# Batches 1 to 7 get their transposed tokens from VectorE blocks and SBUF transfers, and DRAM scratch is laid out in longer rows

## The chip, the cores and the metric

The kernel runs on one core of a Trainium2 chip. The engines named here are TensorE (PE; PEld is its weight load), VectorE (DVE), ScalarE (ACT), GpSimd (POOL) and SyncE (SP), which issues the DMAs of this kernel. The metric is the device time of one execution in microseconds (us), as a median over runs. Data is rearranged on the host before and after the launch, and this is not timed.

## What is computed

The input x has 8 batches of 2048 tokens with 512 features, in float32. The reference, cut to what matters:

```python
xn = _layernorm(x, axis=-1)
q = (xn @ Wq.T + bq).reshape(B, M, 8, 8)
k = (xn @ Wk.T + bk).reshape(B, M, 8, 8)
v = (xn @ Wv.T + bv).reshape(B, M, 8, 64)
scores = einsum('bmhd,bnhd->bhmn', q, k) / sqrt(8)
scores = where(scores >= 0, scores, 0.2 * scores)
out = einsum('bhmn,bnhd->bmhd', softmax(scores), v)
s = gamma * out + xn
base = xn @ W.T                      # feed-forward
ret = ...                            # top-1 of 4 gates per token, its softmax weight
res = sum over 4 experts of ret * (xn @ Wd_i.T) @ Wu_i.T
return x + s * silu(base + res)
```

## The kernel before

A batch's 2048 tokens are cut into 4 blocks of 512 (`BLK`). Two kinds of background work are done per block. `project_block` makes q, k and v from the normalized tokens and writes them to DRAM scratch (QS, KS, VS). `lift_block` makes the feed-forward part and writes it to GS. The main work is attention: for each batch, block of queries and pair of heads (a unit `s`, 128 of them) the inner loop takes 16 steps (`CH`), one per chunk of 128 keys. One step computes scores (`score`, L641), the leaky slope on ACT (`leaky`, L652), subtracts the row maximum with a matmul of two rows (`less_max`, L658), takes the exponential (`exp`, L670), finds maxima for the unit after next (`max_unit`, L586 on PE and L597 on DVE), and adds the exponentials up on POOL (`add_up`, L702). Weighing the values (`weigh`, L682) is put off in a list `last`.

The order of all engines' instructions is the order in which the Python program emits them. Background work consists of generators. Three queues hold them: the ending of a unit, the row shift, and `behind()`, which walks through the list of jobs (projections of batch b + 1 and lifts of batch b, interleaved). Each yield has a label. In each step `half_full()` chooses between weighing up to two chunks and moving a generator on: HOLD means that matmuls into a bank are being accumulated, and two of them fill a step; TINY work goes beside one weighing; WAIT is work that only follows up. A planner gives every job a cost (A1 for a projection, A2 for a lift, MM = 0.86 for one 512-column matmul) and due times (`due_at`), and `spend` counts what has been done; background work is held back once it is 6.0 ahead of the due time. In the last batch `half_light()` does the same in another rhythm.

The tokens' way before. `load_x` brings a block to SBUF (`xt`, two buffers). `norm(b, n)` is a generator that computes the statistics on DVE (L304, L305), the scale and shift on POOL, and issues the first of four normalizations on ACT (L319, into `xn`). It is started one job ahead and moved on only in those steps of `half_full` in which no background matmul is due. `project_block` then transposes the block on PE with 16 matmuls of 128x128 against an identity (L370) in four groups `tp`; each group is copied to `xnT` by DVE (L373) and followed by the next normalization. After the key projection, `split_keys` writes KS and QS (L338, L343), and the normalized tokens XN and the transposed ones XT are stored to DRAM (L389, L390), all on SP. `lift_block` reads XT back (`fetch`, L328). `load_stacks(s + 2)` reads keys and queries in the first steps of a unit (L542, L548), and `max_unit` uses them from step 5 on, since it runs 16 + 11 chunks ahead (`LEAD`). `read_for_ending` reads GS, x and XN for one pair of heads (L713, L715, L716), and `ending` writes the result (L763).

Of the kernel before, what the change touches and what calls it, by code (L numbers as in the profile page):

```python
# [32 lines left out]
def fused_layer_kernel(  # L33
    ctx: ExitStack,
    tc: tile.TileContext,
    x: bass.AP,
    wqk: bass.AP,
# [34 lines left out]
    B, M, C = x.shape  # L72
    NC = C // 128
    NB = M // BLK
# [3 lines left out]
    xv = x.rearrange("b (n p t) c -> b n p t c", p=128, t=NT)  # L78
    ov = out.rearrange("b (n p t) c -> b n p t c", p=128, t=NT)
# [15 lines left out]
    KS = [tc.dram_tile([HEADS, 4, DQK, M], FP, name=f"KS{b}") for b in range(B)]  # L95
    VS = [tc.dram_tile([NPAIR, 128, CH, 128], FP, name=f"VS{b}") for b in range(B)]
    GS = [tc.dram_tile([NB, 128, NT, C], FP, name=f"GS{b}") for b in range(B)]
    XN = [tc.dram_tile([NB, 128, NT, C], FP, name=f"XN{b}") for b in range(B)]
# [6 lines left out]
    def load_x(b, n):  # L105
        xt = two.tile([128, NT, C], FP, name="xt")
        if (b, n) == (0, 0):
            for t in range(NT):
                nc.sync.dma_start(out=xt[:, t, :], in_=xv[b, n][:, t, :])
        else:  # L110
            nc.sync.dma_start(out=xt, in_=xv[b, n])
        xtiles[b, n] = xt
# [146 lines left out]

    def project(ps, wt, xnT):  # L260
        for c in range(NC):
            for part in pieces():
                if c or part.start:
                    yield HOLD
                nc.tensor.matmul(  # L265
                    ps[:, part],
                    lhsT=wt[:, c, :],
                    rhs=xnT[c][:, part],
                    start=(c == 0 and part.start == 0),
                    stop=(c == NC - 1 and part.stop == BLK),  # L270
                )
                spend(MM / len(pieces()))

    def token_major(ps, wt, xnT, t, more=False):
        for c in range(NC):
            for part in pieces():
                if c or part.start:
                    yield HOLD
                nc.tensor.matmul(  # L279
                    ps[:, part],  # L280
                    lhsT=xnT[c][:, t * 128 : (t + 1) * 128],
                    rhs=wt[:, c, part],
                    start=(c == 0 and part.start == 0),
                    stop=(c == NC - 1 and part.stop == BLK and not more),
                )
                spend(MM / len(pieces()))

    def columns(*tiles):
        return [a[:, c, :] for a in tiles for c in range(a.shape[1])]
# [8 lines left out]
    def norm(b, n):  # L298
# [17 lines left out]
        xn = two.tile([128, NT, C], FP, name="xn")  # L316

        def normalize(t):
            nc.scalar.activation(  # L319
                xn[:, t, :], xt[:, t, :], AF.Identity, bias=nmr[:, t : t + 1], scale=rstd[:, t : t + 1]  # L320
            )

        normalize(0)
        normed[b, n] = xn, normalize
# [6 lines left out]
    def split_keys(b, n, ps, hi, lo):  # L331
        nc.vector.tensor_tensor(
            hi.bitcast(I32), ps.bitcast(I32), hi_bits.to_broadcast([128, BLK]), ALU.bitwise_and
        )
        nc.vector.tensor_tensor(lo, ps, hi, ALU.subtract)
        tok = slice(n * BLK, (n + 1) * BLK)
        for j in range(4):
            nc.sync.dma_start(  # L338
                out=KS[b][:, j, :, tok],
                in_=(hi, lo)[j // 2][64:128, :],  # L340
            )
        for j in range(4):
            nc.sync.dma_start(  # L343
                out=QS[b][:, j, :, tok],
                in_=(hi, lo)[j % 2][0:64, :],
            )
# [14 lines left out]
    def project_block(b, n, prefetch):  # L361
# [3 lines left out]
        xn, normalize = normed.pop((b, n))  # L365
        xnT = two.tile([128, NC, BLK], FP, name="xnT")
        for t in range(NT):
            tp = bank([128, NC, 128], "tp")
            for c in range(NC):
                nc.tensor.transpose(tp[:, c, :], xn[:, t, c * 128 : (c + 1) * 128], ident)  # L370
            if t + 1 < NT:
                normalize(t + 1)
            nc.vector.tensor_copy(xnT[:, :, t * 128 : (t + 1) * 128], tp)  # L373
            spend(0.5)
            yield TINY if t + 1 < NT else FREE
        if prefetch:
            fetch(*prefetch)
        nxt = b * NB + n + 2
        if nxt < B * NB:
            load_x(nxt // NB, nxt % NB)  # L380

        ps = bank([128, BLK], "qkps")
        yield from project(ps, wqk_sb, columns(xnT))
# [5 lines left out]
        nc.sync.dma_start(out=XN[b][n], in_=xn)  # L389
        nc.sync.dma_start(out=XT[b][n], in_=xnT)  # L390
# [5 lines left out]
        for t in range(NT):  # L396
            ps = bank([128, C], "vps")
            yield from token_major(ps, wv_sb, columns(xnT), t)
            add_bias(vb, t, ps)
            yield FREE if prefetch or t + 1 < NT else TINY  # L400
# [4 lines left out]
    def lift_block(b, n, prefetch, cols=None):  # L405
# [3 lines left out]
        if not early:  # L409
            if (b, n) not in fetched:  # L410
                fetch(b, n)
            cols = columns(fetched.pop((b, n)))
# [70 lines left out]
        if early:  # L483
            yield EARLY
            fetch(b, n)
            cols = columns(fetched.pop((b, n)))
            if prefetch:
                fetch(*prefetch)
# [20 lines left out]
        g = one.tile([128, NT, C], FP, name="g")  # L509
        for t in range(NT):  # L510
# [7 lines left out]
            nc.vector.scalar_tensor_tensor(g[:, t, :], th, 1.0, ps, ALU.add, ALU.mult)  # L518
            yield SLOW if prefetch or t + 1 < NT else TINY
        nc.sync.dma_start(out=GS[b][n], in_=g)  # L520
# [11 lines left out]
    def load_stacks(s):  # L532
# [7 lines left out]
        for r in range(2):  # L540
            half = slice(2 * STK * r, 2 * STK * (r + 1))
            nc.sync.dma_start(  # L542
                out=kst[s % 3][half, :].bitcast(FP).rearrange("r (c p) -> r c p", p=128),
                in_=KS[b][2 * p : 2 * p + 2].rearrange("e j d (c r p) -> r (e j d) c p", r=2, p=128)[r],
            )
# [160 lines left out]
    def read_for_ending(s):  # L706
# [4 lines left out]
        cols = slice(p * 128, (p + 1) * 128)  # L711
        gs = two.tile([128, NT, 128], FP, name="gs")
        nc.sync.dma_start(out=gs, in_=GS[b][n][:, :, cols])  # L713
        xs = two.tile([128, 2, NT, 128], FP, name="xs")
        nc.sync.dma_start(out=xs[:, 0], in_=xv[b, n][:, :, cols])  # L715
        nc.sync.dma_start(out=xs[:, 1], in_=XN[b][n][:, :, cols])  # L716
        reads[s] = gs, xs

    def ending(s):

        b, p, n = where(s)
        cols = slice(p * 128, (p + 1) * 128)
# [40 lines left out]
        nc.sync.dma_start(out=ov[b, n][:, :, cols], in_=gs)  # L763


    A1, A2, LIFTED, KEYED, VALUED = 20 * MM + 2.0, 24 * MM + 3.7, 1.3, 13.8, 15.0
# [29 lines left out]
    def behind():  # L796
        jobs = [t for t in tasks if t[0]]
        for k, (f, b, n, _, _) in enumerate(jobs):
            g, bb, nn = (jobs[k + 1] if k + 1 < len(jobs) else (None, 0, 0))[:3]
            if g is project_block:  # L800
                stats[bb, nn] = norm(bb, nn)
# [44 lines left out]

    def half_full():
# [8 lines left out]
        if go_on():  # L856
            values(run)
            return
# [3 lines left out]
        if j is not None and state[j] == TINY:  # L862
            values(min(run, 1))
            go(j)
            ended[0] = True
        elif j is None or len(last) > MUCH - (state[j] != HOLD) or (ended[0] and run > 1):
            ended[0] = False
            for g in stats.values():
                next(g, None)
# [32 lines left out]
    with tc.manual_schedule():  # L902
# [5 lines left out]
        def normalize_all(own, n):  # L908
# [5 lines left out]
            nc.sync.dma_start(out=XN[0][n], in_=xn)  # L914

        def turn(n, own, between):

            xn, _ = normed.pop((0, n))
            if n < 2:
                full = two.tile([128, NC, BLK], FP, name="xnT")  # L920
                halves = [full[:, 0:2, :], full[:, 2:4, :]]
# [32 lines left out]
        def value(n, t):  # L954
            if t == 0:
                if n % 2:
                    spare = one.tile([128, NT, C], FP, name="g")
                    vbs[n] = spare.rearrange("p a (b d) -> p a b d", b=NT)
# [40 lines left out]
        for n in range(NB):  # L999
# [123 lines left out]
```

## Time and profile before

| what | us |
|---|---|
| median of three runs | 5593.18 |
| lowest and highest run | 5574.32, 5600.27 |
| span of the profiled execution | 5580.8 |
| TensorE busy in the span | 5338.6 |
| GpSimd busy | 4778.5 |
| ScalarE busy | 4448.0 |
| VectorE busy | 3672.4 |

The profiled execution has its span, from its first instruction to its last, as its own time; no other is given for it. It lies between the lowest and the highest run. The DMA engines are busy 35% of the span, and 615 MB move. In the profile a group of instructions has its line, engine, operation, output and inputs, shapes, count, busy time and the mean time of one in nanoseconds, and then the idle time of the engine before them with what ended it. A list of waits has the waiting engine and line, what released it, and the total us, the number of times and the longest.

### The profile page before, as it was taken

The page shows a single profiled execution, that of the slowest core. Times are in us where ns is not written, and L with a number is a line of the kernel's source. Part 1 is how long each engine was busy: PE and PEld are TensorE (multiplying, and loading weights), DVE is VectorE, ACT ScalarE, POOL GpSimd, SP SyncE. Part 2 cuts the span into 40 slices and gives each one's busy share as a digit, 9 for nine tenths or more (in the row PEclk, how much of TensorE's full clock was granted, in tenths as well). Part 3 has the DMA queues.
Part 4 walks back from the last instruction along what each step waited for, and adds up shares of the span by engine and source line. Part 5 has one row for each costly group of instructions (what it writes and reads, how often), then busy time and mean ns, then how long its engine had stood idle before and what let it go on. Part 6 is the DMA issues. An engine that isn't in the chain of part 4 may idle for free.

```text
span 5580.8 us, 78283 instructions
## 1 busy us (share of the span) xinstructions
PE 5338.6 (96%) x26258; PEld 1975.0 (35%) x26258; DVE 3672.4 (66%) x4990; ACT 4448.0 (80%) x8627; POOL 4778.5 (86%) x2906
## 2 busy tenths in 40 slices
PE   7999999999999999999999999999999999999998
PEld 3333333333333333333333333333333333333332
DVE  5665766667666666667667666676666667666663
ACT  1787888788887788878888788887788878888887
POOL 1887898889897889988899888898889988899898
PEclk9998999999998999999999999999999999999998
DMA  5333343334423343333432334323343242432221
GB/s 191 113 111 114 109 133 97 101 116 120 125 94 95 124 127 111 98 101 124 136 108 88 108 116 152 101 80 117 111 146 95 83 144 88 142 96 84 72 78 61
DMA packets 528265, 615.39 MB, mean 110 GB/s; under 512 B 44092, under 2 KB 438332, under 8 KB 491768
## 3 DMA queue, kind: packets, MB, share of 16 engines
q1 hardware_dynamic: 527864, 610.39, 35.1%
q8 instruction: 209, 3.42, 0.3%
q14 instruction: 192, 1.57, 0.1%
HBM read 407.88 MB, written 202.38 MB: 109 GB/s over the span
## 4 chain that ended last, share of the span: by engine, by line
PE 84%; ACT 8%; DMA 3%; DVE 2%; issue 1%; SPq 1%; POOL 0%; ACTq 0%; POOLq 0%; DVEq 0%
PE av L682 30%; PE sc L658 17%; PE zps L279 9%; PE vps L279 8%; PE mx L586 8%; ACT ex L670 5%; ACT sc L652 3%; DMA q_sb<-QS 2%; PE qkps L265 2%; PE pps L265 2%; PE dps L265 2%; PE atp L754 1%; PE dps L737 1%; PE tp L370 1%; DVE mxr L597 1%
## 5 line engine op out<-in xcount | busy, mean ns | idle before, releaser
L702 POOL TENSOR_TENSOR acc<-acc,ex 128x1024 f32<-128x1024 f32 x1792 | 4231.4, 2361 | 255.3 <-ACT ex L670 138.4
L597 DVE TENSOR_REDUCE mxr<-mx 128x2 f32<-128x1024 f32 x2030 | 2480.0, 1222 | 1209.7 <-PE sc L658 942.8
L670 ACT ACTIVATE ex<-sc 128x512 f32<-128x512 f32 x4096 | 2228.5, 596 | 951.8 <-PE sc L658 831.3
L652 ACT ACTIVATE sc<-sc 128x512 f32<-128x512 f32 x4096 | 2234.4, 591 | 17.9 <-PE sc L641 17.9
L682 PE MATMUL av<-ex,v_sb 128*64 128x512 f32 x8192 | 2140.3, 627 | 4.5 <-DVE avs L724 3.1
L658 PE MATMUL sc<-shift,ones_r 2*128 2x512 f32 x4096 | 1654.7, 462 | 77.7 <-ACT sc L652 65.8
L586 PE MATMUL mx<-k,q_sb 32*128 32x512 f32 x4096 | 1463.2, 453 | 66.3 <-DMA q_sb<-QS 62.4
L658 PEld LDWEIGHTS sc<-shift,ones_r 2*128 2x128 f32 x4096 | 694.8, 187 | 1542.3 <-ACT sc L652 1453.1
L641 PE MATMUL sc<-q_sb,k 32*128 32x512 f32 x4096 | 1036.4, 502 | 0.0
L682 PEld LDWEIGHTS av<-ex,v_sb 128*64 128x64 f32 x8192 | 468.6, 138 | 843.1 <-issue 819.5
L586 PEld LDWEIGHTS mx<-k,q_sb 32*128 32x128 f32 x4096 | 572.6, 187 | 90.5 <-issue 69.8
L279 PE MATMUL zps<-w_sb,xnT 128*128 128x512 f32 (+1 forms) x1120 | 529.0, 589 | 7.5 <-DMA xnT<-XT 7.5
L279 PE MATMUL vps<-wv_sb,xnT 128*128 128x512 f32 x960 | 477.1, 621 | 0.2
L702 POOL TENSOR_TENSOR acc<-ex 128x1024 f32<-128x1024 f32 x128 | 301.8, 2357 | 169.0 <-ACT ex L670 168.7
L641 PEld LDWEIGHTS sc<-q_sb,k 32*128 32x128 f32 x4096 | 385.4, 185 | 0.8 <-issue 0.8
L279 PEld LDWEIGHTS zps<-w_sb,xnT 128*128 128x128 f32 x1120 | 187.0, 190 | 234.9 <-issue 229.7
L279 PEld LDWEIGHTS vps<-wv_sb,xnT 128*128 128x128 f32 x960 | 164.5, 190 | 200.1 <-issue 198.7
L518 DVE SCALAR_TENSOR_TENSOR g<-th,zps 128x512 f32<-128x512 f32 x128 | 88.0, 688 | 185.0 <-ACT th L517 185.0
L611 POOL TENSOR_TENSOR ml<-m,big 128x8 f32<-128x8 f32 x128 | 26.2, 205 | 202.5 <-DVE m L610 196.3
L349 DVE TENSOR_TENSOR vb<-vps,bv_sb 128x512 f32<-128x512 f32 x120 | 82.9, 691 | 93.4 <-PE vps L279 93.2
L373 DVE COPY xnT<-tp 128x512 f32<-128x512 f32 x112 | 77.3, 690 | 97.5 <-PE tp L370 97.5
L265 PE MATMUL dps<-xnT,wd_sb 128*128 128x512 f32 (+1 forms) x280 | 134.4, 592 | 0.0
(124 smaller groups left out, 2717.7 us busy)
## 6 DMA issues: line engine op xcount, KB each, us to landing
v_sb<-VS SPq DMA_DIRECT2D x127, 1024.0 KB
k<-KS SPq DMA_DIRECT2D x256, 256.0 KB
XN<-xn SPq DMA_DIRECT2D x32, 1024.0 KB
q_sb<-QS SPq DMA_DIRECT2D x256, 128.0 KB
xnT<-XT SPq DMA_DIRECT2D x32, 1024.0 KB
GS<-g SPq DMA_DIRECT2D x32, 1024.0 KB
gs<-GS SPq DMA_DIRECT2D x128, 256.0 KB
xs<-in_x_dram SPq DMA_DIRECT2D x128, 256.0 KB
```

The lines of the kernel that those rows point to most:

```text
L265: nc.tensor.matmul(ps[:, part], lhsT=wt[:, c, :], rhs=xnT[c][:, part], start=(c == 0 and part.start == 0), stop=(c == NC - 1 and part.stop ...
L279: nc.tensor.matmul(ps[:, part], lhsT=xnT[c][:, t * 128 : (t + 1) * 128], rhs=wt[:, c, part], start=(c == 0 and part.start == 0), stop=(c = ...
L349: nc.vector.tensor_tensor(vb[:, :, t, :], ps.rearrange("p (h d) -> p h d", h=NPAIR), bv_sb.rearrange("p (h d) -> p h d", h=NPAIR), ALU.add,)
L518: nc.vector.scalar_tensor_tensor(g[:, t, :], th, 1.0, ps, ALU.add, ALU.mult)
L586: nc.tensor.matmul(parts[e], lhsT=q_sb[r, t * 128 : (t + 1) * 128], rhs=k_sb[r, kb // 2 * BLK : (kb // 2 + 1) * BLK], start=True, stop=True,)
L597: nc.vector.reduce_max(mxr[s][:, :, t, kb : kb + 1], mx, axis=AX.X)
L641: nc.tensor.matmul(sc[e], lhsT=k_sb[r, i // 2 * 128 : (i // 2 + 1) * 128], rhs=q_sb[r, :], start=True, stop=True,)
L652: nc.scalar.activation(sc[e], sc[e], AF.Prelu, alpha=SLOPE)
L658: nc.tensor.matmul(sc[e], lhsT=ones_r[r, :], rhs=shifts[s][r, :], start=False, stop=True, skip_group_check=True,)
L670: nc.scalar.activation(ex[:, e, :], sc[e], AF.Exp, scale=qscale)
L682: nc.tensor.matmul(avt[s][64 * e : 64 * e + DV, :], lhsT=v_sb[:, i, 64 * e : 64 * e + DV], rhs=ex[:, e, :], start=(i == 0), stop=(i == CH ...
L702: nc.gpsimd.tensor_tensor(acc[s], old, ex, ALU.add)
```

## The change

For batches 1 to 7 the tokens are no longer transposed on PE. `norm` normalizes in place (`xt`, now with three buffers). DVE transposes each group of 512 features in 32x32 blocks into a tile `xb`, which leaves each block in the wrong group of partitions. Sixteen DMAs from SBUF to SBUF, each from 32 partitions to 32, put the blocks in their place in `xnT`. The host lays out x so that the order of the tokens comes out right. `norm` is started two jobs ahead, and a new function `prepare` moves it on in more kinds of steps. The transfers wait until the job before the projection has begun. XN is then stored with four DMAs, and the next block is loaded at the end of `norm`. `project_block` finds its tokens ready and stores XT only after the third group of values.

In DRAM, KS keeps a row of 1024 keys together, GS and the output are split by pairs of heads, and x comes a second time (`xp`) in that order. XN is in token order. Key stores become eight DMAs in place of four, key loads four in place of two. The first batch still uses PE; its first two blocks stay in SBUF for the first two lifts, so that four half-block XT stores and two reads less are made. The planner's A1 falls by 2.0.

The diff, cut to its core:

```diff
-    KS = [tc.dram_tile([HEADS, 4, DQK, M], FP, name=f"KS{b}") for b in range(B)]
+    KS = [tc.dram_tile([4, HEADS * DQK, 2, M // 2], FP, name=f"KS{b}") for b in range(B)]
-    GS = [tc.dram_tile([NB, 128, NT, C], FP, name=f"GS{b}") for b in range(B)]
-    XN = [tc.dram_tile([NB, 128, NT, C], FP, name=f"XN{b}") for b in range(B)]
+    GS = [tc.dram_tile([NB, NPAIR, 128, NT, 128], FP, name=f"GS{b}") for b in range(B)]
+    XN = [tc.dram_tile([NB, BLK, C], FP, name=f"XN{b}") for b in range(B)]
...
+    def turned_columns(xnT):
+        by_c = xnT.rearrange("p a (c m) -> p c a m", c=NC)
+        return [by_c[:, c] for c in range(NC)]
...
-    def norm(b, n):
+    turn_at = [0]
+    def norm(b, n, job=0):
...
         normalize(0)
-        normed[b, n] = xn, normalize
+        if b == 0:
+            normed[b, n] = xt, normalize
+            return
+        xb = one.tile([128, 4, NC, NT, 32], FP, name="xb")
+        for t in range(NT):
+            yield
+            nc.vector.transpose(
+                xb[:, :, :, t, :].rearrange("p f c i -> p c f i"),
+                xt[:, t, :].rearrange("p (c f j) -> p c f j", c=NC, f=4),
+            )
+            if t + 1 < NT:
+                normalize(t + 1)
+        while turn_at[0] < job - 1:
+            yield
+        xnT = two.tile([128, NC, BLK], FP, name="xnT")
+        for a in range(4):
+            for f in range(4):
+                nc.sync.dma_start(
+                    out=xnT[32 * f : 32 * f + 32, a, :],
+                    in_=xb[32 * a : 32 * a + 32, f].rearrange("j c t i -> j (c t i)"),
+                )
+        fetched[b, n] = xnT
+        yield
+        for t in range(NT):
+            nc.sync.dma_start(
+                out=XN[b][n].rearrange("(a t i) c -> t a i c", a=4, t=NT)[t], in_=xt[:, t, :]
+            )
+        yield
+        nxt = b * NB + n + 2
+        if nxt < B * NB:
+            load_x(nxt // NB, nxt % NB)
...
     def split_keys(b, n, ps, hi, lo):
         for j in range(4):
-            nc.sync.dma_start(
-                out=KS[b][:, j, :, tok],
-                in_=(hi, lo)[j // 2][64:128, :],
-            )
+            keys = (hi, lo)[j // 2][64:128, :].rearrange("k (c r p) -> r k c p", r=2, p=128)
+            for r in range(2):
+                nc.sync.dma_start(
+                    out=KS[b][j, :, r, n * BLK // 2 : (n + 1) * BLK // 2].rearrange("k (c p) -> k c p", p=128),
+                    in_=keys[r],
+                )
...
     def project_block(b, n, prefetch):
         for _ in stats.pop((b, n)):
             pass
-        xn, normalize = normed.pop((b, n))
-        xnT = two.tile([128, NC, BLK], FP, name="xnT")
-        for t in range(NT):
-            tp = bank([128, NC, 128], "tp")
-            for c in range(NC):
-                nc.tensor.transpose(tp[:, c, :], xn[:, t, c * 128 : (c + 1) * 128], ident)
-            if t + 1 < NT:
-                normalize(t + 1)
-            nc.vector.tensor_copy(xnT[:, :, t * 128 : (t + 1) * 128], tp)
-            spend(0.5)
-            yield TINY if t + 1 < NT else FREE
+        xnT = fetched.pop((b, n))
+        cols = turned_columns(xnT)
         if prefetch:
             fetch(*prefetch)
-        nxt = b * NB + n + 2
-        if nxt < B * NB:
-            load_x(nxt // NB, nxt % NB)
...
-        nc.sync.dma_start(out=XN[b][n], in_=xn)
-        nc.sync.dma_start(out=XT[b][n], in_=xnT)
...
+            if t == 2:
+                nc.sync.dma_start(out=XT[b][n], in_=xnT)
...
     def lift_block(b, n, prefetch, cols=None):
         if early:
             yield EARLY
-            fetch(b, n)
-            cols = columns(fetched.pop((b, n)))
-            if prefetch:
-                fetch(*prefetch)
...
-        nc.sync.dma_start(out=GS[b][n], in_=g)
+        nc.sync.dma_start(out=GS[b][n].rearrange("h p t d -> p h t d"), in_=g)
...
     def load_stacks(s):
         for r in range(2):
-            half = slice(2 * STK * r, 2 * STK * (r + 1))
-            nc.sync.dma_start(
-                out=kst[s % 3][half, :].bitcast(FP).rearrange("r (c p) -> r c p", p=128),
-                in_=KS[b][2 * p : 2 * p + 2].rearrange("e j d (c r p) -> r (e j d) c p", r=2, p=128)[r],
-            )
+            for e in range(2):
+                h = 2 * p + e
+                nc.sync.dma_start(
+                    out=kst[s % 3][rows(r, e), :].bitcast(FP),
+                    in_=KS[b][:, h * DQK : (h + 1) * DQK, r, :],
+                )
...
-    A1, A2, LIFTED, KEYED, VALUED = 20 * MM + 2.0, 24 * MM + 3.7, 1.3, 13.8, 15.0
+    A1, A2, LIFTED, KEYED, VALUED = 20 * MM, 24 * MM + 3.7, 1.3, 13.8, 15.0
...
     def behind():
+        begun = set()
         for k, (f, b, n, _, _) in enumerate(jobs):
-            if g is project_block:
-                stats[bb, nn] = norm(bb, nn)
+            turn_at[0] = k
+            for m in (k + 1, k + 2):
+                if m < len(jobs) and jobs[m][0] is project_block and jobs[m][1:3] not in begun:
+                    begun.add(jobs[m][1:3])
+                    stats[jobs[m][1:3]] = norm(*jobs[m][1:3], m)
...
+    def prepare():
+        for g in stats.values():
+            if next(g, g) is not g:
+                break
     def half_full():
         if go_on():
             values(run)
+            prepare()
             return
...
         if j is not None and state[j] == TINY:
             values(min(run, 1))
             go(j)
+            prepare()
             ended[0] = True
         elif j is None or len(last) > MUCH - (state[j] != HOLD) or (ended[0] and run > 1):
             ended[0] = False
-            for g in stats.values():
-                next(g, None)
+            prepare()
             values(run)
```

## The prediction

> **What bounds the kernel now.** I read the page's busy shares first, then its list of line groups, then the waits of TensorE (PE), and last the busy time of single steps of the inner loop, because shares are averages over unlike steps.
>
> ```profile
> span 5580.8 us, 78283 instructions
> PE 5338.6 (96%) x26258; PEld 1975.0 (35%) x26258; DVE 3672.4 (66%) x4990; ACT 4448.0 (80%) x8627; POOL 4778.5 (86%) x2906
> ...
> L702 POOL TENSOR_TENSOR acc<-acc,ex 128x1024 f32<-128x1024 f32 x1792 | 4231.4, 2361 | 255.3 <-ACT ex L670 138.4
> ...
> L373 DVE COPY xnT<-tp 128x512 f32<-128x512 f32 x112 | 77.3, 690 | 97.5 <-PE tp L370 97.5
> ```
>
> PE is the fullest engine. GpSimd (POOL) is next: 2048 steps at 2.36 us are 4833 us, so no saving on PE goes much below some 4900. In the waits of PE only two entries are large and touched by the change, and one single wait:
>
> ```profile
> PE mx L586 <- DMA q_sb<-QS: 62.4, 18, 7.3
> PE tp L370 <- ACT xn L319: 47.0, 28, 1.7
> PE zps L279 <- DMA xnT<-XT: 7.5, 1, 7.5
> ```
>
> (Columns: total us, times, longest.) A step is one pass of the loop over key chunks; on PE it runs from one pair of score matmuls (L641) to the next. The first starts at 132.2 us, so the 2048 steps hold 5448.6 us. Busy time of six stretches (columns: length, then busy PE, PEld, DVE, ACT, POOL, clock, DMA share, GB/s):
>
> ```profile
> 574.00:576.54 2.54, 2.54 (x17) 0.88 (x17) 2.48 (x4) 2.11 (x5) 2.46 (x2) 1.00 0.03 3
> 1857.96:1860.18 2.22, 1.74 (x14) 0.56 (x12) 2.19 (x4) 1.75 (x5) 2.14 (x2) 1.00 0.04 4
> 366.59:370.84 4.25, 2.57 (x14) 1.10 (x15) 2.01 (x3) 4.25 (x8) 4.15 (x2) 1.00 0.46 177
> 382.13:384.39 2.26, 2.26 (x17) 0.92 (x16) 1.40 (x3) 1.73 (x5) 2.26 (x1) 1.00 0.38 112
> 384.39:387.01 2.62, 2.53 (x15) 1.09 (x14) 1.95 (x3) 2.62 (x6) 2.46 (x3) 1.00 0.07 13
> 412.84:420.40 7.56, 1.43 (x10) 0.68 (x6) 1.15 (x4) 0.99 (x2) 1.92 (x1) 0.71 0.99 255
> ```
>
> In order: a step with two chunks weighed (2.54 us); one with a single chunk and no other work (2.22); a block's first four transposes with two normalizations on ScalarE (ACT), 4.25; four transposes and no normalization, 2.26; four with one, 2.62; and a step that waits for q_sb with the DMA engines full. The reader is to see that the transposes hardly lengthen a step (2.26 against 2.22). What lengthens it is the normalization of 0.82 us on ACT, which is full in the third and fifth row, and the wait for it.
>
> **The change, part by part.** The sum is made against the span of 5580.8 us; the three timed runs have the median 5593.2 (5574 to 5600), so the span lies 12 below it and I carry differences over to the median.
>
> Transposes out. Over all steps of the trace, the 112 with tp transposes last 347.0 us: 28 with two normalizations 116.0 (4.14 each), 56 with one 162.6 (2.90), 28 with none 68.4 (2.44). Each also weighs one chunk. The 199 steps with one weighing alone average 2.28. If the 112 become such steps: 347.0 - 112 x 2.28 = 91.6 us less. The planner's cost A1 falls by 2.0 of 19.2, which moves the due times but adds no instruction; priced at 0, its effect on phases is in the DMA term.
>
> Normalizations moved. All 112 stay (0.82 us each, in place now) and go, one per call of prepare, to steps with weighings. ACT spends 2.1 to 2.2 us of a step on scores and exponentials. Lower end 0: a tanh of 0.60 us in a two-chunk step costs nothing (77 steps with it and 485 without, both median 2.54). Upper end 0.82 each (92 us), ACT having no slack. In the transpose steps one normalization costs 2.90 - 2.44 = 0.46. About half the calls fall in two-chunk steps like the tanh's, half in one-chunk steps; I take 0.25: +28 us.
>
> VectorE (DVE). Out go 112 copies of 0.69 us, in come 112 block transposes of 128x512. The trace has only 128x32, 0.201 us; ends are 0.68 (other operations over 512 elements) and 16 x 0.201 = 3.2. A copy of 128x32 takes 0.180 (L479), so the price grows as for other operations and I take 0.7: 0, beside PE work on an engine 66% busy. If that cover went, a DVE burst longer than a step would hold up mx. The g write in another order is like the add of bias (0.691 against 0.688): 0. The transposes wait for ACT's normalization of the call before, a step earlier; queued behind them is the row maximum mxr, for which the next mx waits.
>
> Queues. SP issues in order. A block's key split (from 400.23 us in the first projection) issues 4 KS, 4 QS, XN and XT stores at 0.5 to 1.6 us each until 408.1; only then come the loads of k (2.75) and q (2.79), which land at 419.4, while mx needs them at 413.3. That is the 6.1 us wait, with XN and XT, 1 MB each, ahead of the loads on engines at a share of 1.0. The 7 such waits, one per batch, make 45 of the 62.4 us. After the change XN leaves this place, XT comes some value tiles later, k comes in rows of 4 KB. KS becomes 8 stores, 16 transfers turn the tokens, XN becomes 4: per block 23 DMAs more, some 14 us of SP at 0.6, and 2 k loads more per query block. SP issues for 1406 us in all (25%), so this lies beside other work, unless it stands before a load of stacks, due 5 steps (13 us) after its issue, or before SH and shift. The xnT transfers also wait for the job two back to release its buffer; behind that wait in SP stand the stack loads. Ends: all waits gone, -62; or each of 28 blocks waits 6.5 as the worst now, 182 - 62 = +120. I assume that a quarter of the blocks still meet a load, at half the length since 2 MB are gone from its front, and the small ones stay: -25.
>
> A rule speaks against this part. The store row is L389: one DMA of 0.65 us to issue, in 8 KB rows (0.36 us a packet in the trace's packet records; 2 KB takes 0.113). The Trainium skill ("DMA: Bandwidth & Descriptors", section on why a DMA increments its semaphore by 16) says that a DMA is spread over the largest number up to 16 that divides the slowest dimension of both sides; the new XN stores and k loads have an outer 4 in DRAM, so four engines. By it the XN store would hold four engines 512 / 4 x 0.113 = 14 us, an estimate, and if a quarter of the blocks met that the total would be about 5570; by the row it is nothing. No row here shows which.
>
> Opening and rest. The early lift keeps its columns and does not fetch: the 7.5 us wait goes. Reads of gs and xs and the output in long rows: PE waits for none now: 0; without that cover they cost their 0.6 us of SP. Matmuls over four runs of 128: L737 reads runs of 32 and takes a mean of 410 ns for 256 columns, the contiguous 256 columns of L279 take 424: 0.
>
> Sum: -91.6 + 28 + 0 - 25 - 7.5 = -96. Span 5485, median 5593 - 96 = 5497.
>
> **Rivals.** (1) ACT has no slack: 0.82 for each normalization and unchanged q_sb waits: -91.6 + 92 - 7.5, so 5586, no change. For: ACT is full in the rows above; against: the tanh rows. (2) Slower by SP and the rings: the token transfers and stores stand before the stack loads, mx waits. At 9 us in each block: -96 - 37 + 252, so 5712. It decides from 161 us in waits, 5.8 per block (forecast 37 in all). For: SP is in order, 23 more DMAs a block, the share of 0.99 in such a stretch. Against: 2 MB fewer in front of the loads. (3) Block transposes of 3.2 us: a DVE step of 1.23 + 3.2 = 4.4 against 2.54, 1.9 x 112 = 213: 5710. (4) The change does not do what it says: tokens not ready when a projection starts, so that the rest is drained there: 4 x (0.82 + 0.70) + 16 x 0.6 + 5 for landing = 21 us a block, 5593 - 96 + 580 = 6080. Against: of the 1792 steps before the last batch 1155 hold no projection matmul; in 57 jobs that is 20 calls of prepare a job, and 13 are needed.
>
> **How the numbers follow.** Half a percent (28 us) is what a measurement can tell from no change. Forecast 0.66, rival 1 0.11, rival 2 0.14, rival 3 0.06, rival 4 0.03. The forecast's own range: 5593 - 92 - 62 - 7 = 5432 to 5593 - 92 + 52 + 12 = 5565. The stated range goes from 5432 past rival 1 into rival 2 at 6.4 us a block (-96 - 37 + 179), 5640. Of the forecast and rival 1 together a little can fall on either side of the bound: faster 0.67, same 0.11, slower 0.22.
>
> **What would show it.** Right: no transposes in steps, the steps that replace them near 2.3; ACT rows of 0.82 beside two-chunk steps of about 2.6; block transposes near 0.7; the q_sb wait near 37 us; no wait for xnT at 155 us. Wrong: PE waiting for xnT from xb, for q_sb or shift over 160 us in total, block transposes over 1.5 us, or ACT's normalizations making two-chunk steps of 3.3 us.

## The result and the profile after

| | before | after |
|---|---|---|
| median, us (6 runs each) | 5586.1 | 5916.65 |
| lowest and highest run | 5558.34, 5600.27 | 5914.75, 5957.67 |
| span of the profiled execution | 5580.8 | 5915.3 |
| mean granted clock of TensorE | 0.970 | 0.934 |

The ratio is 1.0614 with a 95% interval of 1.0585 to 1.0642: the changed kernel is slower by 6%, where 1.7% faster was forecast. The page of the profile after, in the rows that answer to those shown of before:

```profile
span 5915.3 us, 78471 instructions
PE 5417.2 (92%) x25810; PEld 1977.3 (33%) x25810; DVE 3648.9 (62%) x4990; ACT 4446.7 (75%) x8627; POOL 4777.9 (81%) x2906
```

TensorE has 448 matmuls less and is busy 79 us longer, yet for 92% of the span in place of 96%. Its waits (total us, times, longest):

```profile
PE mx L619 <- DMA q_sb<-QS: 281.1, 22, 21.0
PE sc L691 <- ACT sc L685: 128.1, 294, 2.0
PE sc L691 <- DMA shift<-SH: 34.7, 9, 5.3
```

Before, the first was 62.4, and the other two were

```profile
PE sc L658 <- ACT sc L652: 65.8, 192, 0.5
PE sc L658 <- DMA shift<-SH: 5.3, 1, 5.3
```

The waits of the transposes for ACT (47.0) and the wait for xnT in the opening (7.5) are gone. The two rows of the moved work in the list of line groups:

```profile
L327 ACT ACTIVATE xt<-xt,nmr,rstd 128x512 f32<-128x512 f32 x128 | 104.8, 828 | 11.5 <-POOL nmr L323 11.2
L338 DVE STREAM_TRANSPOSE xb<-xt 128x512 f32<-128x512 f32 x112 | 78.5, 701 | 3.6 <-DMA SH<-cT 1.9 <-ACT sc L685 1.5 <-issue 0.2
```

Where the largest wait comes from is seen in stretches around it (columns: length, busy PE, PEld, DVE, ACT, POOL, granted clock, DMA share, GB/s):

```profile
399.00:403.00 4.00, 4.00 (x26) 1.32 (x22) 2.60 (x4) 3.13 (x8) 3.92 (x2) 1.00 0.45 107
420.00:422.00 2.00, 1.72 (x11) 0.33 (x5) 0.64 (x2) 1.29 (x4) 1.92 (x2) 1.00 0.25 55
422.00:424.00 2.00, 0.00 (x0) 0.00 (x0) 0.00 (x0) 0.41 (x1) 0.84 (x1) 1.00 0.26 96
426.00:428.00 2.00, 0.00 (x0) 0.00 (x0) 0.00 (x0) 0.00 (x0) 0.00 (x0) 0.50 0.99 401
434.00:438.00 4.00, 0.00 (x0) 0.00 (x0) 0.00 (x0) 0.00 (x0) 0.00 (x0) 0.50 0.90 241
438.00:442.00 4.00, 0.00 (x0) 0.00 (x0) 0.00 (x0) 0.00 (x0) 0.00 (x0) 0.50 0.26 96
447.00:455.00 8.00, 8.00 (x28) 2.56 (x28) 5.42 (x8) 4.12 (x8) 6.43 (x3) 0.50 0.01 2
```

And the chain that ended last, in the same place (start, us, what):

```profile
406.16 1.65 DMA shift<-SH
...
418.59 11.43 DMA XN<-xt
430.04 12.57 DMA q_sb<-QS
```

SP issues, in order: the 16 token transfers, the last 15 of them from 395.6 to 406.1 us, most at 0.59 each and one at 1.38; loads of the shift and for the ending; eight KS and four QS stores from 409.2 to 417.1; four XN stores until 420.9; the load of the next block, which takes 3.36 to issue; and only from 424.4 the four loads of k, then those of q. Before, the same loads were issued from 408.2 to 413.8. While the XN stores and, at the end, the loads run, the DMA share stands at 0.25 and 0.26: a quarter of the 16 engines. The chain puts 11.43 us on the third XN store, from its issue to its landing, and 12.57 on the second load of q, which SP issues only when that store has landed (SP waits 2.0 us for it). PE stands still until 442.74, 21.0 us, against 6.1 before, and its clock is still at half speed until 455. Each of the seven batches with projections repeats this, with waits of 18 to 21, 11 to 14 and 6 to 8 us for q_sb and one of 3 to 5 for shift.

To see where all of the time went, every step of the inner loop is split three ways: idle time of PE of over 0.5 us in front of an instruction ("waits"); for the steps of which over 2% ran below full clock, what then lies over 2.54 us, the mean step at full clock ("clock"); and the rest, work at full clock, which still holds the waits of up to 0.5 us. "Half clock" is all the time for which the trace shows 0.50. Worked out from the records of the traces, in us:

| kernel | waits | clock | work | steps in all | first step at | half clock |
|---|---|---|---|---|---|---|
| before | 132.4 | 113.2 | 5203.0 | 5448.6 | 132.2 | 340.5 |
| after | 367.2 | 209.2 | 5198.1 | 5774.5 | 140.8 | 787.8 |

The 334.5 us of the two spans are 234.8 of waits, 96.0 of lower clock, 8.6 of a later first step (3.9 of it a wait for q_sb at 84.7 us that is new), and -4.9 of work.

### The profile page after: what moved, and what is told of

Same layout as the page of the kernel before. It is cut to its first block, busy times and chain, and to the rows that moved or that the text cites. A ratio compares the mean times of both kernels' runs of the same rounds, so it can differ in the third digit from the quotient of the medians.

```text
span 5915.3 us, 78471 instructions
## 1 busy us (share of the span) xinstructions
PE 5417.2 (92%) x25810; PEld 1977.3 (33%) x25810; DVE 3648.9 (62%) x4990; ACT 4446.7 (75%) x8627; POOL 4777.9 (81%) x2906
## 3 DMA queue, kind: packets, MB, share of 16 engines
q8 instruction: 205, 3.36, 0.2%
## 4 chain that ended last, share of the span: by engine, by line
PE 76%; DMA 9%; ACT 8%; DVE 4%; issue 1%; SPq 1%; POOL 1%; ACTq 0%; POOLq 0%; DVEq 0%
PE av L715 28%; PE sc L691 16%; PE zps L282 9%; PE vps L282 7%; PE mx L619 7%; ACT ex L703 5%; DMA q_sb<-QS 4%; ACT sc L685 3%; DMA XN<-xt 2%; PE pps L268 2%; PE qkps L268 2%; DMA SH<-cT 1%; PE atp L785 1%; PE dps L268 1%; DMA xs<-in_xp_dram 1%
## 5 line engine op out<-in xcount | busy, mean ns | idle before, releaser
L715 PE MATMUL av<-ex,v_sb 128*64 128x512 f32 x8192 | 2173.0, 636 | 3.1 <-DVE avs L755 0.3
L691 PE MATMUL sc<-shift,ones_r 2*128 2x512 f32 x4096 | 1689.1, 469 | 163.8 <-ACT sc L685 128.1
L619 PE MATMUL mx<-k,q_sb 32*128 32x512 f32 x4096 | 1480.9, 463 | 295.0 <-DMA q_sb<-QS 281.1
L691 PEld LDWEIGHTS sc<-shift,ones_r 2*128 2x128 f32 x4096 | 713.8, 190 | 1740.4 <-ACT sc L685 1583.5
L674 PE MATMUL sc<-q_sb,k 32*128 32x512 f32 x4096 | 1054.0, 510 | 0.0
L282 PE MATMUL zps<-w_sb,xnT 128*128 128x512 f32 (+1 forms) x1120 | 565.4, 624 | 0.0
L282 PE MATMUL vps<-wv_sb,xnT 128*128 128x512 f32 x960 | 497.4, 643 | 0.2
L674 PEld LDWEIGHTS sc<-q_sb,k 32*128 32x128 f32 x4096 | 391.4, 188 | 0.8 <-issue 0.8
L755 DVE COPY avs<-av 128x512 f32<-128x512 f32 x128 | 87.9, 687 | 86.5 <-PE av L715 85.4
```

The source lines that it names most:

```text
L282: nc.tensor.matmul(ps[:, part], lhsT=xnT[c][:, t], rhs=wt[:, c, part], start=(c == 0 and part.start == 0), stop=(c == NC - 1 and part.stop ...
L619: nc.tensor.matmul(parts[e], lhsT=q_sb[r, t * 128 : (t + 1) * 128], rhs=k_sb[r, kb // 2 * BLK : (kb // 2 + 1) * BLK], start=True, stop=True,)
L674: nc.tensor.matmul(sc[e], lhsT=k_sb[r, i // 2 * 128 : (i // 2 + 1) * 128], rhs=q_sb[r, :], start=True, stop=True,)
L691: nc.tensor.matmul(sc[e], lhsT=ones_r[r, :], rhs=shifts[s][r, :], start=False, stop=True, skip_group_check=True,)
L715: nc.tensor.matmul(avt[s][64 * e : 64 * e + DV, :], lhsT=v_sb[:, i, 64 * e : 64 * e + DV], rhs=ex[:, e, :], start=(i == 0), stop=(i == CH ...
L755: nc.vector.tensor_copy(avs, avt.pop(s))
```

## The experiments

Two theories stood at first. R: transfers confined to a few DMA engines (the XN stores and the k loads, each with an outer dimension of 4 in DRAM) hold the rings (the queues of the DMA engines) when the stacks are due. S: it is the number and the order of the transfers on SP, above all the 16 in one burst. In the later runs F carries on R, and O carries on S. Ratios are to the kernel before, on the same chip.

**The XN stores over 32 partitions each.** As many stores, bytes and rows of 2 KB; each store now takes 32 partitions with all their rows, so that the outermost dimension is 32 and not 4.

```diff
-        for t in range(NT):
-            nc.sync.dma_start(
-                out=XN[b][n].rearrange("(a t i) c -> t a i c", a=4, t=NT)[t], in_=xt[:, t, :])
+        for a in range(4):
+            nc.sync.dma_start(
+                out=XN[b][n].rearrange("(a t i) c -> a i t c", a=4, t=NT)[a], in_=xt[32 * a : 32 * a + 32])
```

> The changed kernel with the four XN stores cut by groups of 32 partitions instead of by token group, so that the outer dimension in DRAM is 32 rows and not 4. Number and bytes of the DMAs stay. Theory R (rings): the XN stores use a quarter of the DMA engines (share 0.25 from 419 to 423 us of the changed kernel) and the loads behind them wait; then the waits of mx for q_sb fall from 281 us to below 130, shift waits from 35 to below 15, and the time from 5917 to 5700 to 5780. Theory S (SP): the loads are late because SP has to issue 33 DMAs of 0.6 us before them (395 to 424 us); then the waits stay above 230 us and the time above 5850.

Measured: 5770.5, ratio 1.0352 (1.0246 to 1.0457); the q_sb waits fall from 281.1 to 179.0, those for shift from 34.7 to 5.5. The time is in R's range, the waits lie between the two.

```profile
PE mx L619 <- DMA q_sb<-QS: 179.0, 23, 16.1
```

In the stretches that hold the XN stores, the share is no longer a quarter:

```profile
416.00:418.00 2.00, 2.00 (x14) 0.71 (x10) 1.52 (x3) 1.84 (x5) 1.92 (x2) 1.00 0.96 224
418.00:420.00 2.00, 1.01 (x7) 0.19 (x3) 0.00 (x0) 1.00 (x2) 2.00 (x1) 1.00 0.96 239
```

So the confinement to four engines is real, and lifting it takes off 146 us of the 330; it is not the whole.

**Keys as before.** KS, its stores and its loads are those of the kernel before: four stores, two loads.

```diff
-    KS = [tc.dram_tile([4, HEADS * DQK, 2, M // 2], ...)]
+    KS = [tc.dram_tile([HEADS, 4, DQK, M], ...)]
...
-            for e in range(2):
-                nc.sync.dma_start(out=kst[s % 3][rows(r, e), :]..., in_=KS[b][:, h * DQK : (h + 1) * DQK, r, :])
+            nc.sync.dma_start(out=kst[s % 3][half, :]..., in_=KS[b][2 * p : 2 * p + 2]...[r])
```

> The changed kernel with the key scratch, its four stores and its two loads as before the change. SP issues 4 DMAs less per block and 2 less per query block. Theory R: the new key loads stand on four engines too, 4 x 128 KB, about 6 us of those engines; without them q_sb waits fall by some 60 to 100 us of 281, time 5810 to 5860. Theory S: 2.4 us less of SP per block in front of the loads, at most 28 x 2.4 = 67 us less, time 5850 to 5900. If the long rows of keys were the gain they look like, the waits rise.

Measured: 5783.0, ratio 1.0374 (1.0279 to 1.0470), shift waits 16.0.

```profile
PE mx L616 <- DMA q_sb<-QS: 167.9, 14, 16.6
```

The time is below both ranges: the new layout of the keys costs 134 us, more than either theory gave it. The edit takes back three things at once, the outer 4 of the loads, their number and that of the stores; no run parts them.

**Spread.** The 16 transfers go in four groups and the XN stores one by one, each at a call of `prepare` of its own.

```diff
         for a in range(4):
             for f in range(4):
                 nc.sync.dma_start(out=xnT[32 * f : 32 * f + 32, a, :], ...)
+            if a < 3:
+                yield
...
         for t in range(NT):
             nc.sync.dma_start(out=XN[b][n]...[t], in_=xt[:, t, :])
+            yield
```

> The changed kernel with the 16 token transfers issued in four groups of four and the four XN stores one by one, each group in its own call of prepare, so in different steps; nothing else differs. Theory S: other DMAs get between them, q_sb waits fall from 281 to below 120 us, time 5680 to 5770. Theory R: the XN stores still hold four engines 14 us a block; with pauses between them the loads wait less but not nothing: 130 to 230 us, time 5760 to 5860.

Measured: 5741.3, ratio 1.0299 (1.0194 to 1.0405).

```profile
PE mx L622 <- DMA q_sb<-QS: 119.7, 24, 8.3
```

Both marks are those of S: with the same four-engine transfers, 175 us go when they no longer come in one burst. The three savings, each alone, make 455 us of a loss of 330, so they overlap. The added yields also move the normalizations: of the 105 steps that hold one, 70 lay at the gate's matmuls or within three steps behind them in the changed kernel, and 20 do here. The waits for ACT fall with that from 128.1 to 108.3, a small part of the 175.

**The layouts alone.** All tokens are transposed by PE as before, with `norm` started one job ahead; XN is one store over 16 engines; the new layouts stay.

```diff
-        xnT = fetched.pop((b, n))
-        cols = turned_columns(xnT)
+        xn, normalize = normed.pop((b, n))
+        for t in range(NT):
+            ...                      # four transposes on PE, the next normalization, the copy
+        cols = columns(xnT)
```

> The DRAM layouts of the change (keys, GS, output, xp, XN in token order with one store of 16 engines) and the first batch as changed, but the tokens of all batches transposed on PE as before, normalized at the old place, one job ahead. Theory R and S both: no burst, q_sb waits at 40 to 110 us, time 5560 to 5640, within 1% of before. If the layouts by themselves were the loss (key loads on four engines, eight key stores), waits above 200 us and 5800 or more.

Measured: 5728.2, ratio 1.0276 (1.0175 to 1.0377). Both theories had it at 5560 to 5640: a miss for both. Its waits:

```profile
PE mx L603 <- DMA q_sb<-QS: 128.8, 23, 9.7
PE sc L675 <- ACT sc L669: 64.8, 192, 0.8
PE tp L380 <- ACT xt L327: 47.0, 28, 1.7
```

The second and third row are those of the kernel before; the first has doubled.

**The layouts, with keys as before.** The run before, with the edit on KS.

> The layouts alone, with the tokens transposed by TensorE as before, and in addition the keys' array KS, its stores and its loads as before. Left of the change: GS, XN, the xp array and the output in long rows, XT stored after the third value group. Theory F (transfers confined to four engines and cut into more pieces delay the stacks, so the keys' layout is what the layouts alone lost): within 1% of the kernel before, 5530 to 5630, q_sb waits of 30 to 75 us. Theory O (the order and number of transfers matter, not the keys' rows): still 1.5% or more above before, over 5660, q_sb waits over 100 us.

Measured: 5538.1, ratio 0.9927 (0.9899 to 0.9955); the row above falls to

```profile
PE mx L600 <- DMA q_sb<-QS: 27.5, 7, 4.5
```

F holds, down to a wait a little under its range. The keys' layout is the loss of the layouts, 190 us in this pair; the other long rows show no cost. The loads of the keys can be seen alone in the first batch, a stretch of the layouts alone first, then one of the kernel before:

```profile
186.00:188.00 2.00, 2.00 (x8) 0.76 (x9) 1.14 (x1) 1.79 (x4) 1.92 (x2) 1.00 0.26 98
185.00:186.00 1.00, 1.00 (x10) 0.19 (x8) 0.27 (x1) 0.93 (x2) 1.00 (x1) 1.00 0.60 176
```

In rows of 4 KB they run at a share of 0.26, in rows of 512 bytes at 0.60.

**Both mended.** The changed kernel with the XN stores and the keys of the first two runs.

> The changed kernel with the keys as before and the XN stores cut so that each runs over 32 partitions. Theory F: the two savings add up (133 and 146 us alone, from 5917): 5620 to 5690, q_sb waits below 110 us. Theory O (the 16 token transfers and their place in front of the loads are the rest of it): 5690 to 5770, q_sb waits of 110 us or more.

Measured: 5634.3, ratio 1.0101 (1.0069 to 1.0134), q_sb waits 69.4. The two savings add up (146 + 134 = 280; 282 measured). F holds; the kernel is still 1% above before.

**Both mended and spread.**

> As the run before, and the 16 token transfers in four groups and the XN stores one by one, each group at a call of prepare of its own. Theory F+O: with all three causes out, what is left is the work taken from TensorE: 5500 to 5610, q_sb waits of 30 to 80 us. Theory A (the normalizations, moved into steps with a softmax of the gate, hold up TensorE and bring the lower clock by themselves): 5620 to 5700 although the q_sb waits fall below 80 us, with half clock for over 500 us.

Measured: 5533.1, ratio 0.9914 (0.9880 to 0.9948). The waits for q_sb are gone, where F+O left 30 to 80 us, and those for ACT stand first:

```profile
PE sc L691 <- ACT sc L685: 112.1, 286, 1.5
...
PE mx L619 <- DMA q_sb<-QS: 0.8, 2, 0.5
```

With the three causes out, the change is 0.9% faster than before. But it is no faster than the layouts with keys as before and PE transposing (0.9927): the work taken from PE shows nowhere. Half clock still takes 391 us. Theory A's 5620 is not reached, so A does not hold in that size; spreading has itself left only 21 of the 105 steps with a normalization near the gate's matmuls. What A names can be seen in the trace of the changed kernel:

```profile
597.28:600.66 3.38, 1.75 (x14) 0.50 (x13) 2.83 (x11) 2.50 (x6) 3.22 (x3) 0.90 0.01 1
603.76:607.87 4.11, 4.11 (x19) 1.52 (x17) 2.36 (x6) 3.50 (x6) 3.95 (x3) 0.50 0.64 192
613.99:618.85 4.86, 4.86 (x13) 1.67 (x11) 1.36 (x2) 2.45 (x5) 3.74 (x2) 0.50 0.32 115
```

The first is a step after the gate's softmax with a normalization on ACT: PE waits 1.63 us in it. The clock goes to 0.50, and the next steps take 3.1 to 5.2 us. The kinds of step of the second and third row (the gate's `rps` matmuls beside a weighing; four lift matmuls) average 2.58 and 2.75 us over the trace of before.

**Late stores, in the kernel before.** One edit to the kernel before.

```diff
         split_keys(b, n, ps, hi, lo)
-        nc.sync.dma_start(out=XN[b][n], in_=xn)
-        nc.sync.dma_start(out=XT[b][n], in_=xnT)
...
             add_bias(vb, t, ps)
+            if t == 2:
+                nc.sync.dma_start(out=XN[b][n], in_=xn)
+                nc.sync.dma_start(out=XT[b][n], in_=xnT)
```

> The kernel before with one edit: the stores of XN and XT go out after the third value group, not between the split of the keys and the loads. It measures what a wait for the stacks costs with the lower clock behind it. Theory C (a wait costs its length and as much again in clock): q_sb waits from 62 to 15 to 30 us, and the time 60 to 110 us below before. Theory L (a wait costs its length only): 30 to 50 us below. If the stores meet other loads instead: no change.

Measured: 5509.8, ratio 0.9874 (0.9823 to 0.9925), so 42 to 99 us less, with fewer waits than the 15 to 30 us that C had left.

```profile
PE mx L587 <- DMA q_sb<-QS: 3.4, 4, 1.7
```

The waits fell by 59.0 us and the span by 62.6. C and L can't be told apart by this: the time fits C, while the span fell by hardly more than the waits. The slow steps behind waits for DMA did become fewer, but others appeared elsewhere (in all 113.2 and 108.3 us).

**Calm.** As both mended and spread, and the second to fourth normalization only beside weighings with no other work.

```diff
             if t + 1 < NT:
+                while not calm[0]:
+                    yield
                 normalize(t + 1)
...
         elif j is None or len(last) > MUCH - (state[j] != HOLD) or (ended[0] and run > 1):
             ended[0] = False
+            calm[0] = True
             prepare()
+            calm[0] = False
```

> The last version of the changed kernel (keys as before, XN stores over 32 partitions, everything spread), and the second to fourth normalization of a block only at calls of prepare beside a step with weighings and no other work, no longer beside the gate's softmax. Theory A (these normalizations hold up the scores of the softmax steps, 112 us of waits for ACT against 66 in the kernel before, and bring 391 us of half clock): waits for ACT back to 65 to 80 us, half clock below 330 us, the time 5470 to 5515. Theory T (the lower clock comes from the lighter steps as such): no change, 5520 to 5545, half clock over 360 us.

Measured: 5479.3, ratio 0.9816 (0.9785 to 0.9846), half clock 289 us. Time and clock are those of theory A. The total of the waits for ACT is not, where 65 to 80 was expected:

```profile
PE sc L694 <- ACT sc L688: 108.6, 291, 1.0
```

Only their length changed, from 1.5 us to 1.0 at most. That this is what the clock answered to is not shown, for the block transposes left the gate's steps with the normalizations (22 of the 112 lay there, now 1).

**Layouts with keys as before, late XN.** PE transposes; the XN store goes behind the third value group, beside that of XT.

> The layouts alone with the keys as before, tokens transposed by TensorE, and the store of XN moved behind the third value group too. Beside the kernel before with late stores (5510) it tells what the long rows of GS, XN, xp and the output are worth by themselves. Theory F and theory C: nothing, as PE waits for none of them, 5495 to 5525. If shorter transfers free the rings for the stacks: 5460 to 5495.

Measured: 5498.1, ratio 0.9850 (0.9824 to 0.9876), against 0.9874 (0.9823 to 0.9925) for late stores with the old layouts: the long rows of GS, XN, xp and the output are worth nothing that these runs can show.

**The same with the normalizations one job ahead.** PE still transposes, but the four normalizations come in `norm`, one at each call of `prepare`, in the steps where the changed kernel calls it.

```diff
         normalize(0)
+        if b:
+            for t in range(1, NT):
+                yield
+                normalize(t)
         normed[b, n] = xt, normalize
...
-            if t + 1 < NT:
-                normalize(t + 1)
             nc.vector.tensor_copy(xnT[:, :, t * 128 : (t + 1) * 128], tp)
```

> As the run before, tokens still transposed by TensorE, but all four normalizations of a block one job ahead, one at each call of prepare, and prepare called where the changed kernel calls it. Beside the changed kernel with its three transfers mended (5533) it tells the transposes from the normalizations. Theory N (the 112 steps were long by the normalizations, and a transpose on TensorE costs next to nothing): the waits of the transposes for ACT go from 47 to about 0, the 112 steps take 2.3 to 2.5, the time is 5440 to 5500, at or below the changed kernel mended. Theory V (the transposes themselves cost): 5510 to 5560, above the changed kernel mended less its half clock.

Measured: 5439.5, ratio 0.9748 (0.9711 to 0.9784), at the lower edge of theory N. In the list of line groups the copies stand as before, the transposes take a little less than in the row of before, which comes last here, and their wait of 47.0 us is gone:

```profile
L383 DVE COPY xnT<-tp 128x512 f32<-128x512 f32 x112 | 77.0, 688 | 32.1 <-PE tp L382 32.1
L382 PE MATMUL tp<-ident,xt 128*128 128x128 f32 x448 | 73.5, 287 | 0.0
L370 PE MATMUL tp<-ident,xn 128*128 128x128 f32 x448 | 81.8, 311 | 47.0 <-ACT xn L319 47.0
```

The 112 steps with transposes now last 274.3 us (2.45 each), against 347.0.

**Normalizations ahead and calm, in the kernel before.** Old layouts, late stores, PE transposes, and the edit above with the calm rule for the second to fourth normalization.

> The kernel before, layouts untouched, with the stores of XN and XT late and the normalizations one job ahead and kept out of the gate's softmax steps. If theories N and A both hold, the fastest of all: 5420 to 5480, waits for ACT in the scores near 65 us, half clock below 330 us. If what is saved comes back as waits or lower clock: 5490 to 5520, as with late stores alone.

Measured: 5435.7, ratio 0.9738 (0.9709 to 0.9768): the lowest, 2.6% below the kernel before and 8% below the changed one, with none of the change's transfers. The run before, with the long rows and without the calm rule, lies within its interval, so neither difference is worth anything that these runs can show. The page, and the largest wait of PE:

```profile
span 5433.4 us, 78143 instructions
PE 5288.2 (97%) x26258; PEld 1974.3 (36%) x26258; DVE 3662.6 (67%) x4990; ACT 4445.3 (82%) x8627; POOL 4778.0 (88%) x2906
...
PE sc L667 <- ACT sc L661: 72.0, 203, 1.1
```

The split of the steps for the runs that decide, made as in the first table:

| kernel | waits | clock | work | half clock |
|---|---|---|---|---|
| before | 132.4 | 113.2 | 5203.0 | 340.5 |
| after | 367.2 | 209.2 | 5198.1 | 787.8 |
| layouts alone | 186.2 | 211.7 | 5197.9 | 599.3 |
| layouts, keys as before | 94.2 | 97.1 | 5200.2 | 288.7 |
| both mended | 131.5 | 154.1 | 5201.7 | 497.2 |
| both mended and spread | 39.4 | 142.5 | 5201.5 | 391.4 |
| the same, calm | 31.5 | 103.3 | 5202.4 | 288.8 |
| layouts, late XN, normalizations ahead | 37.4 | 79.9 | 5214.4 | 230.4 |
| before, late stores, normalizations ahead, calm | 28.8 | 53.5 | 5217.6 | 163.1 |

The reader is to see the column of work: it stays within 5198 and 5218 in all of them, with 448 transposes on PE or without. But for these 20 us and at most 9 of a later first step, all that any of these kernels gained or lost lies in waits and clock.

## Why the prediction was wrong

The step that failed is the term of the queues, taken at -25 us with ends of -62 and +120.

- **Queues.** Measured: q_sb waits from 62.4 to 281.1 and shift from 5.3 to 34.7, +248 us, twice the upper end. (What the term assumes comes to -23, not -25, which is of no weight.) The mechanism is that of the second rival, with its own mark passed: 161 us of waits were to decide, and there were 316 (11.3 per block where it priced 9). Its 5712 was too low as well, by 205 us, for it kept the other terms of the sum and priced no lower clock. Three assumptions carried the wrong value. "By the row it is nothing": the row was a DMA of other shape, and the XN stores held a quarter of the engines, 11.43 us in the chain. "k comes in rows of 4 KB" was counted as neutral or a help; with its stores and loads it cost 134 us in the changed kernel and 190 in the layouts alone, where the loads with an outer 4 ran at a share of 0.26. "This lies beside other work": 10.5 us of token transfers, 7.9 of key and query stores and 3.8 of XN stores, all on SP, stood ahead of the loads in the same steps, because `prepare` reaches them while the neighbouring projection is at its own stores.
- **The rule that spoke against this part.** The row is the share of 0.25 and 0.26 above, and 0.96 with 32 partitions outermost. The Trainium skill ("DMA: Bandwidth & Descriptors", section on why a DMA increments its semaphore by 16) gives four engines for an outer dimension of 4; the trace agrees. The estimate of 14 us worked out from it for the XN stores stands against 11.43 measured from the third one's issue to its landing. The estimate of 5570 made with it was too low, as it left out the k loads, which have the same outer 4, and how the transfers lie in time.
- **The price of a wait.** The prediction priced a wait at its length alone. Taken over all waits of PE for a DMA of 2.5 us or more, one was followed within 30 us by a mean of 7.5 to 13.5 us at half clock, and the unbroken run of slow steps behind it lost 3.0 to 4.2 us by it, in each of the eight kernels with eight or more such waits (before, after, the first six runs). The mean length of these waits shows no effect: 4.1 us (layouts, keys as before) cost 3.0, 10.7 us (after) 3.5. No term of the sum held that; 57 of the 96 us of clock lie there (29 such waits in place of 11).
- **Transposes out (-91.6).** The 47 us of waits went as forecast. The other 45 did not: at full clock and without waits of over 0.5 us, the 591 steps with a single weighing, projection matmuls or transposes came to 1446.6 us before, and the 592 in their place to 1432.4, which is 14 less. The 112 were compared with steps of a single weighing, 2.28. There are 78 more of those (2.20 in this count), but also 36 with two projection matmuls beside a weighing, of which there were none (2.87), and 34 with two projection matmuls alone in place of 35 with four. And the term belonged to the normalizations: with these moved and PE still transposing, the 112 steps fall by 73 of the 92 us. A group of four transposes adds 2.45 - 2.22 = 0.23 us to a step with one weighing, 26 us in all.
- **Normalizations (+28, ends 0 and 92).** The waits for ACT rose by 62.3 us. The 0.25 for each came from tanh beside two weighings, but 70 of the 105 steps with a normalization lie at the gate's matmuls or within three steps behind them, where DVE and ACT do many short instructions (11 on DVE in the row of 3.38 us) and PE waits for the scores. Keeping them out of there took 54 us off the spread version (5533.1 to 5479.3), in which 21 of the 105 still lay there.
- **Block transposes (0.7 each).** 0.701: right, and PE's waits for DVE's row maximum rose only from 2.1 to 11.3 us. The wait for xnT in the opening went, also as forecast, though the first step starts 8.6 us later.
- **The other rivals.** ACT without slack (5586) names part of what happened, with 62 of its 92 us. Block transposes of 3.2 us and tokens that are not ready did not occur: PE never waited for xnT from xb.

The stated range missed too: its upper bound, 5640, allows 6.4 us of waits per block and nothing for the clock.

What stays open: in the mended and calm version, 249 of the 289 us at half clock begin with no wait of PE over 1 us before them. 225 of the 289 begin in a step with the gate's matmuls or within 10 us behind it, stretches that make 20% of the span, though no normalization lies there any more. What starts them was not tried.

## What to carry to other kernels

Before work is taken off the fullest engine, look at what makes those steps long: here it was an elementwise instruction on ScalarE one step too late, and moving that alone gave 59 us (5498.1 to 5439.5) with the transposes left on PE, most of what their removal was to give. The price of a DMA here did not follow its bytes or the length of its rows: look at how many pieces its outermost dimension allows and at what stands behind it in its queue when a load is due. A wait of the critical engine should be priced with the clock that it costs afterwards, here 3 to 4 us for each long one.

## What was not expected of the hardware

- In the changed kernel PE waited 13 times for ACT for 1.44 to 1.99 us, and each time 6.8 to 24 us at half clock lay in the 35 us behind; in the calm version no such wait is left. The Trainium skill ("TensorE: Matmul & The Clock Gate", Part 1) has, in its table of the two states, the clock fall after at least one idle window of about 3.4 us and rise after one busy window of that length. The runs here differ from that table: in the changed kernel the clock fell at these waits without an idle time of that length, and the 8 us from 447 to 455 ran at 0.50 with PE busy throughout.
- Issuing a DMA on SP is not of fixed cost in these traces. The token transfers took a median of 0.59 us and up to 1.88; the load of the next block took a median of 0.45 us before and 2.35 after, up to 3.95, when it came behind the XN stores; with these over 32 partitions it took a median of 0.58.
- Transfers from SBUF to SBUF of 32 partitions, one after the other from SP, reached a DMA share of 0.45 and 107 GB/s in the stretch from 399 to 403 us.
